# All of B's casts on GpSimd, the first group's second layer moved forward, and a fixed order for the last node blocks: a graph-network kernel on one Trainium2 core

## The chip, the cores and the metric

The kernel runs on one NeuronCore of a Trainium2 chip. A core has a matrix engine (TensorE, called PE), VectorE (DVE), ScalarE (ACT), GpSimd (POOL) and SyncE (SP, which here only starts transfers), each with its own instruction stream, which it works through in order; they meet through semaphores. Sixteen DMA engines move data between the chip's large memory (HBM) and the on-chip memory; results of PE land in PSUM[...]. The metric is the device time of a run in microseconds (us); lower is better.

## The reference

There are 6250 nodes with 128 features each (`x`) and 100000 edges from `src` to `dst`, sorted by `dst`. All arithmetic is float32.

```
h   = relu(concat(x[src], x[dst]) @ Wm1 + bm1)      # 256 wide
h   = relu(h @ Wm2 + bm2)                           # 256 wide
m   = h @ Wm3 + bm3                                 # 128 wide, a message per edge
agg = segment_sum(m, dst) / clip(count(dst), 1)     # mean of messages per node
upd = relu(concat(x, agg) @ Wn1 + bn1) @ Wn2 + bn2
out = layernorm(x + (x + upd))                      # no gain or bias, eps 1e-5
```

## The kernel before

**Tables.** `Wm1` is split in two: A = x @ Wm1[:128] and B = x @ Wm1[128:] are computed once per node rather than once per edge, and written to HBM. A row of A (`atab`) is 256 float32. A row of B (`btab`) is three bfloat16 parts whose sum is the float32 value. The nodes are 49 tiles of 128, in 13 blocks of up to four tiles. A loop (PE's order in it is written out by hand) does for each block: `turn`, which transposes x on PE (L263) into `xT`; `a_table` for pairs of tiles (product L232, copy from PSUM by ACT L241, write to HBM by SP L242); and three blocks later `b_table`. In `b_table` a pair of tiles costs: product (PE, L232), first bfloat16 part (ACT, L249), remainder `rest` (DVE, L250), second part, a cast of `rest` (L252 on POOL for the first 36 tiles, L254 on ACT for the others), third part (DVE, L255), and the write (SP, L256). The other engines are ordered by a scheduler that places instructions by its own estimate of times; where a block is marked as manually scheduled for an engine, that engine keeps the program's order.

**The node products of x.** `x @ Wn1[:128] + bn1` is also computed ahead, by `x_part`: two 128x512 products on PE per block of nodes (L316), each moved out of PSUM by ACT (L318) or DVE (L320), into the space of `xT` and `x_sb`. Four lists say where each of the 13 blocks is done: X_BESIDE between the last B products, X_BEHIND after them, X_FIRST beside the first groups of edges, X_END beside the last ones.

**Edges.** 100000 edges are 196 groups of 512. For each group `fetch` gathers 4 x 128 rows of A on POOL's queue (L412, one indirect DMA per 128 rows; they need all of `atab`) and loads the windows of B rows that the sorted destinations touch on SP's queue (L418; they need all of `btab`). There are four buffers of each. `hot` makes 0/1 matrices on DVE (L433, L436). `first_layer` adds, in PSUM, the transposed A rows (L449) and B windows times 0/1 (L455), and ACT applies the ReLU (L460). `second_layer` multiplies by Wm2 (L469) and DVE applies bias and ReLU (L471). `sums` adds the edges of a window (L478), `add_up` transposes that and DVE adds it to `acc` (L489, L494), which POOL set to zero before (L376). In PE's order a group's second layer stands after the next group's first layer.

**Nodes.** `acc` is turned into the output by 15 node blocks: the 106 odd nodes, two half blocks of 256, ten of 512, two of 256. `products` (L671, L673, L676), `hidden` (L685 to L687) two blocks ahead of `norm`. `norm` multiplies on PE (`pot`, L698, two PSUM buffers), adds 2x (`y`, DVE, L703), takes mean and variance (`bn_stats`, `bn_aggr`, L707, L708), the square root on ACT (`sd`, L710), reciprocal and shift on DVE (`rs` L712, `sh` L714), and the scaled result `o` by ACT, one instruction per 128 nodes (L718), which SP writes out (L721). `y`, `mv`, `sd` and `o` have two buffers each.

Of the kernel before, what the change touches and what calls it, by code (L numbers as in the profile page):

```python
# [27 lines left out]
def kernel(  # L28
# [122 lines left out]
    with tc.tile_pool(name="prep", bufs=1) as prep, tc.tile_pool(  # L151
# [71 lines left out]
        BLOCKS = -(-NT // 4)  # L223
        BEHIND = 3
        INDICES = 6
        LATE = BLOCKS - 4
        xu = xT, x_sb.rearrange("p t d -> p (t d)")

        def products(t0, m, k):
# [14 lines left out]
        def b_table(t0):  # L244
            m = min(2, NT - t0)
            pbt = products(t0, m, 1)
            bt = brow.tile([P, 2 * 3 * H], BF16, name="bt").rearrange("p (t c h) -> p t c h", t=2, c=3)
            rest = brow.tile([P, 2, H], F32, name="rest", bufs=2)
            nc.scalar.copy(bt[:, :m, 0], pbt[:, :m])  # L249
            nc.vector.tensor_sub(rest[:, :m], pbt[:, :m], bt[:, :m, 0])  # L250
            if t0 < 4 * LATE:
                nc.gpsimd.tensor_copy(bt[:, :m, 1], rest[:, :m])  # L252
            else:
                nc.scalar.copy(bt[:, :m, 1], rest[:, :m])  # L254
            nc.vector.tensor_sub(bt[:, :m, 2], rest[:, :m], bt[:, :m, 1])  # L255
            nc.sync.dma_start(btab[t0 * P:(t0 + m) * P].rearrange("(t p) c h -> p t c h", p=P), bt[:, :m])  # L256

        def turn(t0):
            m = min(4, NT - t0)
            pt = pp.tile([P, 4, P], F32, name="pt", tag="pp")  # L260
            for i in range(m):
                n = min(P, N - (t0 + i) * P)
                nc.tensor.transpose(pt[:, i, :n], x_sb[:n, t0 + i, :], ident[:n, :n])  # L263
            w = min(m * P, N - t0 * P)
            block = xT[:, t0 * P:t0 * P + w]
            if m == 4:
                nc.scalar.copy(block.rearrange("p (n i) -> p i n", i=4), pt)
            else:
                nc.scalar.copy(block, pt[:, 0, :w])
# [53 lines left out]
        def whole(steps):  # L323
            for _ in steps:
                pass
# [3 lines left out]

        X_BESIDE, X_BEHIND, X_FIRST, X_END = [0, 1, 2], [3, 4, 5, 6, 7, 8], [9, 12], [10, 11]
        assert sorted(X_BESIDE + X_BEHIND + X_FIRST + X_END) == list(range(BLOCKS))

        turn(0)
        for i in range(BLOCKS + BEHIND):
            if i + 1 < BLOCKS:
# [26 lines left out]
        dst_row = dst.rearrange("(o e) -> o e", o=1)  # L364
        early = [destinations(2 * k, 2, dst_row) for k in range(3)]

        turns = ExitStack()
        turns.enter_context(tc.manual_schedule(engines={ENG.DVE, ENG.Activation}))
        for b in X_BEHIND:
            whole(x_part(b, bank_pb, (nc.scalar, nc.vector)))  # L370


        PIECE = NPAD // 8
        for c in range(HC + 1):
            for k in range(8):
                nc.gpsimd.memset(acc[:, c, k * PIECE:(k + 1) * PIECE], 0.0)  # L376


        pb3 = pp.tile([P, 1], F32, name="pb3", tag="pp")
# [15 lines left out]
    with edge, tc.tile_pool(name="wk", bufs=2) as wk, tc.tile_pool(  # L395
# [136 lines left out]
        for i in range(NG + ahead + 1):  # L532
            if i == 6:
                turns.close()
            if i == 16:
                late_loads()
                none = wk.tile([16, (NG * GE - E) // 16], I32, name="none", bufs=1)
                nc.vector.memset(none, NONE)
                nc.sync.dma_start(dpad[:E].rearrange("(p e) -> p e", p=16), dst.rearrange("(p e) -> p e", p=16))
                nc.sync.dma_start(dpad[E:].rearrange("(p e) -> p e", p=16), none)  # L540
            for step, after in enumerate((20, 24, 27)):
                if i >= after and (i - after) % 8 == 0 and (i - after) // 8 < len(pieces):
                    double((i - after) // 8, step)
            if i < NG:
                nt = GT if i < NGF else LT
                firsts = load_bases(tilei[0:1, i * GT:(i + 1) * GT], nt, ENG.SP)
                if i == NGF:
                    dbs = last_destinations()
                elif i % 2 == 0:
                    dbs = early.pop(0) if early else destinations(i, min(2, NGF - i), dst_row)  # L550
                st[i] = dict(nt=nt, got=fetch(srcT[:, i, :], nt, firsts), db=dbs.pop(0))
            g = i - ahead
            if 0 <= g < NG:
                s = st[g]
                ag, bw = s.pop("got")

                def make_hot(g):
                    s = st[g]
                    hots[g], s["oh"] = hot(s.pop("db"), pbase[:, g, :], dloc[:, g, :s["nt"]], s["nt"])

                if g not in hots:
                    make_hot(g)
                oht = hots.pop(g)
            k = g - lag - 1
            if 0 <= k < NG:
                s = st.pop(k)
                if "firsts" not in s:
                    s["firsts"] = load_bases(tilei[0:1, k * GT:(k + 1) * GT], s["nt"], ENG.DVE)
                add_up(s["part"], s["firsts"], s["nt"])
            if 0 <= g < NG:  # L570
                s = st[g]
                s["h1"] = first_layer(ag, bw, oht, s["nt"])
                if first:

                    make_hot(g + 1)
                    whole(x_part(first.pop(0), bank_p2, (nc.scalar, nc.vector)))
            k = g - lag
            if 0 <= k < NG:
                s = st[k]
                s["part"] = sums(s["oh"], s["h2"], s["nt"])  # L580
            m = g - 1
            if 0 <= m < NG:
                s = st[m]
                s["h2"] = h2s[m % NH2]
                second_layer(s["h1"], s["h2"], s["nt"])
# [59 lines left out]
    with tc.tile_pool(name="nd", bufs=2) as nd, tc.tile_pool(name="nr", bufs=1) as nr, tc.tile_pool(  # L645
# [33 lines left out]
        def hidden(b, agg):  # L679
            n0, n1 = nodes_of[b]  # L680
            w = n1 - n0
            u = nd.tile([P, HC, NB], F32, name="u", bufs=4)
            for c in range(HC):
                put = pu.tile([P, NB], F32, name="put")
                nc.tensor.matmul(put[:, :w], wu1[:, 1, c * P:(c + 1) * P], agg[:, :w], start=True, stop=True)  # L685
                nc.vector.tensor_add(u[:, c, :w], put[:, :w], xu[c][:, n0:n1])  # L686
                nc.scalar.activation(u[:, c, :w], u[:, c, :w], AF.Relu)  # L687
            return u

        def norm(b, u):  # L690
# [11 lines left out]
            y = nd.tile([P, 4, D], F32, name="y")  # L702
            nc.vector.tensor_add(y[:r, :k, :], x2[:r, :k, :], pot[:r, :k, :])  # L703
            st = nd.tile([P, 4, 6], F32, name="st")
            mv = nd.tile([P, 4, 2], F32, name="mv")
# [3 lines left out]
            sd = nd.tile([P, 4], F32, name="sd")  # L709
# [4 lines left out]
            nc.vector.scalar_tensor_tensor(sh[:r, :k], mv[:r, :k, 0], -1.0, rs[:r, :k],  # L714
                                           op0=ALU.mult, op1=ALU.mult)
            o = nd.tile([P, 4, D], F32, name="o")
            for i in range(k):
                nc.scalar.activation(o[:r, i, :], y[:r, i, :], AF.Identity, bias=sh[:r, i:i + 1],  # L718
                                     scale=rs[:r, i:i + 1])
# [6 lines left out]
        FORE, BACK = 4, 2  # L726
        aggs = {b: products(b) for b in range(FORE)}
        us = {}
        for b in range(B + BACK):
            if b < B:  # L730
                us[b] = hidden(b, aggs.pop(b))
            if b >= BACK:
                norm(b - BACK, us.pop(b - BACK))
            if b + FORE < B:
                aggs[b + FORE] = products(b + FORE)


# [27 lines left out]
```

## Time and profile before

| | |
|---|---|
| time, median of 3 runs | 1451.67 us (1450.17 to 1451.95) |
| the profiled execution: its own time | 1208.8 us |
| its span, first to last instruction | 1207.0 us |
| mean granted PE clock in it | 0.996 |
| busy: PE, DVE, ACT, POOL | 1178.5, 670.4, 454.5, 804.9 us |
| loads, tables and x products (start to the first group) | 0 to 84 us |
| edge groups | 84 to about 1129 us |
| node blocks | 1129 to 1207 us |

The profile is of one execution, and that execution took 1208.8 us, not 1451.67. Durations from it can be summed against 1208.8 only. In a timeline line the first number is the start in us from the start of the span, the second the time from the first start to the last end of the merged instructions, then the engine, the line of the kernel, the operation with output and inputs, the count, and in brackets how long the engine was idle before it and what it waited for. In a table of stretches each engine has its busy time and its number of instructions, then come the granted PE clock (1.00 is full), the busy share of the DMA engines and GB/s.

### The profile page before, as it was taken

The numbers are of one execution on the slowest core, as the hardware profiler recorded it, in microseconds if no ns is written. First come the engines' busy times: TensorE is split into PE (matmuls) and PEld (weight loads), VectorE is DVE, ScalarE is ACT, GpSimd is POOL, SyncE is SP. The second block draws the span as 40 slices with busy tenths as digits, with TensorE's granted clock in tenths as the row PEclk, the third lists the DMA queues.
The fourth block names the chain that finished last, engine by engine and source line by source line (L and its number), as shares of the span: only waits on it lengthen the run. The fifth ranks groups of instructions, "written<-read, shape, count | busy, mean of one in ns | idle before, by whom it ended". The sixth has DMA issues, their size and how long they took to land. (4 is left out here: it accounts for less than half of the span.)

```text
span 1207.0 us, 32797 instructions
## 1 busy us (share of the span) xinstructions
PE 1178.5 (98%) x11196; PEld 895.0 (74%) x11197; DVE 670.4 (56%) x2080; ACT 454.5 (38%) x1163; POOL 804.9 (67%) x859
## 2 busy tenths in 40 slices
PE   7989999999999999999999999999999999999896
PEld 6747777777777777777777777777777777777565
DVE  5864555555555555555555555555555555555586
ACT  5663333333333333333333333333333333333256
POOL 8267777777777777777777777777777777673220
PEclk9999999999999999999999999999999999999999
DMA  8886666666555555555555555555555555552343
GB/s 279 293 261 174 189 180 183 189 191 177 154 151 146 152 153 153 150 152 153 149 148 152 154 154 150 149 152 146 152 153 153 152 152 150 146 148 63 97 111 105
DMA packets 173672, 193.66 MB, mean 160 GB/s; under 512 B 30844, under 2 KB 145486, under 8 KB 173488
## 3 DMA queue, kind: packets, MB, share of 16 engines
q0 software_dynamic: 37984, 103.35, 31.1%
q1 hardware_dynamic: 106956, 61.93, 17.7%
q10 hardware_dynamic: 28564, 26.27, 8.1%
q8 instruction: 90, 1.47, 0.5%
q14 instruction: 78, 0.64, 0.2%
HBM read 168.92 MB, written 22.88 MB: 159 GB/s over the span
## 5 line engine op out<-in xcount | busy, mean ns | idle before, releaser
L412 POOL DMA_INDIRECT ag<-atab,srcT x784 | 752.8, 960 | 282.4 <-issue 184.3
L469 PE MATMUL ph<-w,h 128*128 128x256 f32 x3128 | 727.5, 386 | 1.0 <-ACT x_sb L318 1.0
L469 PEld LDWEIGHTS ph<-w,h 128*128 128x128 f32 x3128 | 578.1, 190 | 152.2 <-DVE acc L494 68.2
L460 ACT ACTIVATE h<-ph,b 128x256 f32<-128x256 f32 x782 | 306.3, 474 | 675.9 <-PE ph L455 495.3
L471 DVE TENSOR_TENSOR h<-ph,nb 128x512 f32<-128x512 f32 x391 | 270.2, 692 | 413.6 <-PE ph L469 411.1
L494 DVE TENSOR_TENSOR acc<-acc,pt 128x63 f32 x782 | 171.7, 220 | 33.9 <-PE ph L455 2.6
L449 PE MATMUL ph<-ident,ag 64*128 64x64 f32 x3128 | 130.3, 223 | 0.6 <-DVE b L382 0.6
L478 PE MATMUL pg<-h,oh 128*32 128x257 f32 x1564 | 125.6, 392 | 0.0
L449 PEld LDWEIGHTS ph<-ident,ag 64*128 64x128 f32 x3128 | 113.5, 139 | 2.7 <-ACT x_sb L318 1.4
L433 DVE TENSOR_SCALAR oht<-db,pbase 128x128 bf16<-128x128 int32 x392 | 104.9, 341 | 1.3 <-PE ph L455 1.0
L489 PEld LDWEIGHTS pt<-ident,part 64*128 64x128 f32 x1173 | 50.9, 136 | 65.9 <-issue 65.2
L455 PE MATMUL ph<-oht,bw 64*128 64x128 bf16 x1564 | 76.6, 217 | 2.7 <-DMA bw<-btab 2.3
L481 ACT COPY part<-pg 128x257 f32<-128x257 f32 x196 | 76.5, 390 | 4.0 <-PE pg L478 4.0
L489 PE MATMUL pt<-ident,part 64*128 64x64 f32 x1173 | 77.8, 238 | 0.2 <-DVE acc L494 0.2
L436 DVE TENSOR_TENSOR oh<-iota_n,dloc 128x128 f32<-128x128 f32 x196 | 55.0, 280 | 20.6 <-PE pg L478 19.7
L676 POOL TENSOR_TENSOR agg<-total,rc 128x512 f32<-128x512 f32 (+2 forms) x15 | 16.0, 1070 | 69.1 <-DVE total L673 65.1
L455 PEld LDWEIGHTS <-bw 64*128 64x128 bf16 x1564 | 53.6, 96 | 3.3 <-DMA bw<-btab 2.6
L232 PE MATMUL pbt<-w,xT 128*128 128x256 f32 x196 | 48.7, 394 | 2.5 <-ACT bt L241 1.6
L478 PEld LDWEIGHTS pg<-h,oh 128*32 128x32 f32 x1564 | 30.8, 108 | 21.7 <-issue 0.8
L232 PEld LDWEIGHTS pbt<-w,xT 128*128 128x128 f32 x196 | 36.8, 197 | 10.9 <-ACT bt L241 2.8
L252 POOL CAST bt<-rest 128x512 bf16<-128x512 f32 x18 | 12.2, 686 | 27.1 <-DVE rest L250 18.0
L698 PEld LDWEIGHTS pot<-wu,u 128*128 128x128 f32 (+1 forms) x196 | 24.0, 191 | 5.5 <-issue 4.8
(109 smaller groups left out, 418.2 us busy)
## 6 DMA issues: line engine op xcount, KB each, us to landing
bw<-btab SPq DMA_DIRECT2D x782, 32.0 KB
db<-in_dst_dram ACTq DMA_DIRECT2D x194, 128.0 KB
ag<-atab,srcT POOLq DMA_INDIRECT x784
btab<-bt SPq DMA_DIRECT2D x24, 384.0 KB
atab<-bt SPq DMA_DIRECT2D x24, 256.0 KB
xd<-in_x_dram SPq DMA_DIRECT2D x12, 256.0 KB
x2tab<-xd SPq DMA_DIRECT2D x12, 256.0 KB
x_sb<-in_x_dram SPq DMA_DIRECT2D x5, 512.0 KB
```

What stands on the lines that cost most here:

```text
L232: nc.tensor.matmul(pbt[:, a, :], xT[:, (t0 + a) * P:(t0 + a + 1) * P], w1[:, k, :], start=True, stop=True)
L412: nc.gpsimd.indirect_dma_start(out=ag[:, j, :], out_offset=None, in_=atab[:, :], in_offset=bass.IndirectOffsetOnAxis(ap=idx[:, j:j + 1], a ...
L433: nc.vector.tensor_scalar(oht[:n, k, :], db[:n, k * P:(k + 1) * P], pb_cols[:n, k:k + 1], None, op0=ALU.is_equal)
L449: nc.tensor.matmul(phs[h][:, c, u * NQ:(u + 1) * NQ], ag[halves[h], u, c * P:(c + 1) * P], ident[halves[h], halves[h]], is_transpose=True, ...
L455: nc.tensor.matmul(phs[h][:, c, k * P:(k + 1) * P], bw[halves[h], k, c * P:(c + 1) * P], oht[halves[h], k, :], start=False, stop=True, ski ...
L460: nc.scalar.activation(h1[:, c, h * 2 * P:(h + 1) * 2 * P], phs[h][:, c, :], AF.Relu, bias=b1[:, c:c + 1])
L469: nc.tensor.matmul(ph2[:, a, :], h1[:, c, (j0 + a) * P:(j0 + a + 1) * P], w2[:, c, :], start=(c == 0), stop=(c == HC - 1))
L471: nc.vector.tensor_tensor(h2[:, j0:j0 + 2, :H], ph2, nb2.to_broadcast([P, 2, H]), op=ALU.max)
L478: nc.tensor.matmul(pg[j * WN:(j + 1) * WN, :], oh[:, j, :], h2[:, j, :], start=True, stop=True, skip_group_check=True)
L481: nc.scalar.copy(part[:n, :], pg[:n, :])
L489: nc.tensor.matmul(pt[:, c, :], rows, ident[halves[h], halves[h]], is_transpose=True, start=True, stop=True, skip_group_check=True)
L494: nc.vector.tensor_add(window, window, pts[j // 2][:, :, k:k + WB])
```

## The change

Four edits:

1. The second part of B is cast by POOL for all tiles (the ACT variant for the last 13 tiles goes). POOL gets the program's order from the tables on, and the zeroing of `acc` stands ahead of the loop: POOL does all 24 memsets, then all 25 casts, then the gathers. In the kernel before, 3 of the memsets stood between the first casts, and POOL had 18 casts.
2. X_BESIDE loses a block (3 to 2), X_BEHIND keeps six, X_FIRST gets the block: one block beside the first group and two (a full one and the 106 odd nodes) beside the second. There the first product is now moved by DVE and the second by ACT.
3. The second layer of group 0 comes directly after its first layer and the x block, ahead of the first layer of group 1. From group 2 on the order is as before.
4. The last node blocks: `norm` is cut into `moments` (to mean and variance), `deviation` (square root) and `scaled` (the rest). `y`, `mv`, `sd` and `o` get three buffers. For the last three blocks DVE and ACT follow the program's order, in which the moments of a block stand ahead of the scaling of the block before, and some of the `o` instructions are done by DVE.

PE, SP and the gathers execute the same instructions as before; ACT loses 7 casts of B and 3 of the last 8 `o` tiles, POOL gains the casts, DVE the tiles.

```diff
-        LATE = BLOCKS - 4
...
-            if t0 < 4 * LATE:
-                nc.gpsimd.tensor_copy(bt[:, :m, 1], rest[:, :m])
-            else:
-                nc.scalar.copy(bt[:, :m, 1], rest[:, :m])
+            nc.gpsimd.tensor_copy(bt[:, :m, 1], rest[:, :m])
...
-        X_BESIDE, X_BEHIND, X_FIRST, X_END = [0, 1, 2], [3, 4, 5, 6, 7, 8], [9, 12], [10, 11]
+        X_BESIDE, X_BEHIND, X_FIRST, X_END = [0, 1], [2, 3, 4, 5, 6, 7], [[8], [9, 12]], [10, 11]
...
+        PIECE = NPAD // 8
+        for c in range(HC + 1):
+            for k in range(8):
+                nc.gpsimd.memset(acc[:, c, k * PIECE:(k + 1) * PIECE], 0.0)
+        turns = ExitStack()
+        turns.enter_context(tc.manual_schedule(engines={ENG.Pool}))
         turn(0)
         for i in range(BLOCKS + BEHIND):
...
-        turns = ExitStack()
         turns.enter_context(tc.manual_schedule(engines={ENG.DVE, ENG.Activation}))
         for b in X_BEHIND:
             whole(x_part(b, bank_pb, (nc.scalar, nc.vector)))
-        PIECE = NPAD // 8
-        for c in range(HC + 1):
-            for k in range(8):
-                nc.gpsimd.memset(acc[:, c, k * PIECE:(k + 1) * PIECE], 0.0)
...
                 if first:
                     make_hot(g + 1)
-                    whole(x_part(first.pop(0), bank_p2, (nc.scalar, nc.vector)))
+                    for b in first.pop(0):
+                        whole(x_part(b, bank_p2, (nc.vector, nc.scalar)))
...
-            m = g - 1
-            if 0 <= m < NG:
+            m = g - 1 if g else g
+            if 0 <= m < NG and "h2" not in st[m]:
...
-            o = nd.tile([P, 4, D], F32, name="o")
-            for i in range(k):
-                nc.scalar.activation(o[:r, i, :], y[:r, i, :], AF.Identity, bias=sh[:r, i:i + 1],
-                                     scale=rs[:r, i:i + 1])
+            o = nd.tile([P, 4, D], F32, name="o", bufs=3)
+            for i, eng in zip(range(k), engines):
+                if eng is nc.scalar:
+                    eng.activation(o[:r, i, :], y[:r, i, :], AF.Identity, bias=sh[:r, i:i + 1], scale=rs[:r, i:i + 1])
+                else:
+                    eng.tensor_scalar(o[:r, i, :], y[:r, i, :], rs[:r, i:i + 1], sh[:r, i:i + 1],
+                                      op0=ALU.mult, op1=ALU.add)
...
+        with tc.manual_schedule(engines={ENG.DVE, ENG.Activation}):
+            us[B - 1] = hidden(B - 1, aggs.pop(B - 1))
+            ends = [(B - 3, [nc.scalar, nc.scalar, nc.scalar, nc.vector]), (B - 2, [nc.scalar, nc.vector]),
+                    (B - 1, [nc.vector, nc.scalar])]
+            before = None
+            for b, engines in ends:
+                y, mv = moments(b, us.pop(b))
+                sd = deviation(b, mv)
+                if before:
+                    scaled(*before)
+                before = b, y, mv, sd, engines
+            scaled(*before)
```

More of the change, by code (lines that the diff above doesn't have):

```diff
@@ L328, in bank_pb @@
             return pb.tile([P, 2, H], F32, name="pxu", tag="pbt")
-        X_BESIDE, X_BEHIND, X_FIRST, X_END = [0, 1, 2], [3, 4, 5, 6, 7, 8], [9, 12], [10, 11]
-        assert sorted(X_BESIDE + X_BEHIND + X_FIRST + X_END) == list(range(BLOCKS))
+        X_BESIDE, X_BEHIND, X_FIRST, X_END = [0, 1], [2, 3, 4, 5, 6, 7], [[8], [9, 12]], [10, 11]
+        assert sorted(X_BESIDE + X_BEHIND + sum(X_FIRST, []) + X_END) == list(range(BLOCKS))
+        PIECE = NPAD // 8
[4 more added lines that the diff above has]
+        turns.enter_context(tc.manual_schedule(engines={ENG.Pool}))
         turn(0)
@@ L688, in hidden, with moments @@
             return u
-        def norm(b, u):
+        def moments(b, u):
             n0, n1 = nodes_of[b]
@@ L701, in norm @@
             nc.sync.dma_start(x2[:r, :k], x2tab[n0:n1, :].rearrange("(t p) d -> p t d", p=r))
-            y = nd.tile([P, 4, D], F32, name="y")
+            y = nd.tile([P, 4, D], F32, name="y", bufs=3)
             nc.vector.tensor_add(y[:r, :k, :], x2[:r, :k, :], pot[:r, :k, :])
             st = nd.tile([P, 4, 6], F32, name="st")
-            mv = nd.tile([P, 4, 2], F32, name="mv")
+            mv = nd.tile([P, 4, 2], F32, name="mv", bufs=3)
             for i in range(k):
@@ L708, in norm, with deviation, scaled @@
                 nc.vector.bn_aggr(mv[:r, i, :], st[:r, i, :])
-            sd = nd.tile([P, 4], F32, name="sd")
-            nc.scalar.activation(sd[:r, :k], mv[:r, :k, 1], AF.Sqrt, bias=eps[:r])
+            return y, mv
+        def deviation(b, mv):
+            r = min(P, nodes_of[b][1] - nodes_of[b][0])
+            k = -(-(nodes_of[b][1] - nodes_of[b][0]) // P)
+            sd = nd.tile([P, 4], F32, name="sd", bufs=3)
+            nc.scalar.activation(sd[:r, :k], mv[:r, :k, 1], AF.Sqrt, bias=eps[:r])
+            return sd
+        def scaled(b, y, mv, sd, engines):
+            n0, n1 = nodes_of[b]
+            k = -(-(n1 - n0) // P)
+            r = min(P, n1 - n0)
             rs = nd.tile([P, 4], F32, name="rs")
@@ L728 @@
         us = {}
-        for b in range(B + BACK):
-            if b < B:
-                us[b] = hidden(b, aggs.pop(b))
+        for b in range(B - 1):
+            us[b] = hidden(b, aggs.pop(b))
             if b >= BACK:
-                norm(b - BACK, us.pop(b - BACK))
+                y, mv = moments(b - BACK, us.pop(b - BACK))
+                scaled(b - BACK, y, mv, deviation(b - BACK, mv), [nc.scalar] * 4)
             if b + FORE < B:
                 aggs[b + FORE] = products(b + FORE)
+        assert BACK == 2
+        with tc.manual_schedule(engines={ENG.DVE, ENG.Activation}):
[10 more added lines that the diff above has]
+            scaled(*before)
 _INS = ['x', 'src', 'dst', 'L0_gnn_Wm1', 'L0_gnn_bm1', 'L0_gnn_Wm2', 'L0_gnn_bm2', 'L0_gnn_Wm3',
```

## The prediction

> **What bounds the kernel now.** I read the engine shares first, then the table of stretches, then PE's timeline where PE is not full, then what those waits hang on.
>
> ```profile
> span 1207.0 us, 32797 instructions
> PE 1178.5 (98%) x11196; PEld 895.0 (74%) x11197; DVE 670.4 (56%) x2080; ACT 454.5 (38%) x1163; POOL 804.9 (67%) x859
> ```
>
> The table of stretches (PE, PEld, DVE, ACT, POOL busy, granted clock, DMA share, GB/s), at the change from tables to groups and at the end:
>
> ```profile
> 75.00:90.00 15.00, 12.09 (x52) 5.47 (x50) 7.44 (x23) 6.28 (x12) 11.58 (x12) 0.97 0.75 225
> 90.00:105.00 15.00, 13.62 (x121) 10.55 (x121) 6.10 (x17) 4.46 (x13) 10.94 (x13) 0.92 0.53 147
> 1190.00:1200.00 10.00, 6.84 (x54) 6.33 (x52) 7.79 (x42) 7.51 (x22) 0.00 (x0) 1.00 0.36 107
> 1200.00:1207.00 7.00, 0.00 (x0) 0.00 (x0) 1.55 (x9) 2.85 (x8) 0.00 (x0) 0.62 0.25 75
> ```
>
> PE is busy 98%: the 1045 us of edge groups are PE's, and the change leaves them alone. PE is idle 28.5 us in all; 7.2 of these wait for the first loads. What can be won lies in three places: the change from tables to groups (idle 2.9 + 1.4 us, and a clock under 1), the 2 us at 1130, and the end (3.2 us, then 7.0 us with no matmul). The change touches the first and the third.
>
> PE's timeline at the first of them, and two single microseconds of the same stretch:
>
> ```profile
> 72.61 10.55 PE L316 MATMUL pxu<-xT,wu 128*128 128x512 f32 x24
> 84.06 0.71 PE L449 MATMUL ph<-ident,ag 64*128 64x64 f32 x16 [0.57 <-DVE b L382]
> 85.91 0.23 PE L455 MATMUL ph<-oht,bw 64*128 64x128 bf16 x1 [1.13 <-DMA bw<-btab]
> 87.34 0.53 PE L455 MATMUL ph<-oht,bw 64*128 64x128 bf16 x7 [1.20 <-DMA bw<-btab]
> 87.80 2.63 PE L316 MATMUL ph<-xT,wu 128*128 128x512 f32 x4
> 93.79 3.72 PE L469 MATMUL ph<-w,h 128*128 128x256 f32 x16 [1.01 <-ACT x_sb L318]
> ```
> ```profile
> 89.00:90.00 1.00, 1.00 (x2) 0.00 (x0) 0.00 (x0) 1.00 (x3) 0.88 (x1) 0.50 0.83 207
> 91.00:92.00 1.00, 1.00 (x19) 0.80 (x16) 0.86 (x4) 0.07 (x1) 0.70 (x2) 0.50 0.49 153
> ```
>
> What stands behind that stall on SP, DVE and POOL:
>
> ```profile
> 83.05 17.13 SPq L418 DMA_DIRECT2D bw<-btab  x23
> 78.20 0.43 DVE L255 TENSOR_TENSOR bt<-rest,bt 128x256 bf16<-128x256 f32 x1 [0.64 <-ACT bt L254]
> 83.14 0.08 DVE L538 MEMSET none<- 16x22 int32 x1 [0.91 <-DMA btab<-bt]
> 66.94 1.05 POOL L412 DMA_INDIRECT ag<-atab,srcT  x1 [2.58 <-DMA atab<-bt]
> ```
>
> PE ends the x products at 83.2, and group 0's last B window lands only at 87.34. The windows are issued from 83.05, when all of `btab` is written, and the last part of `btab` left DVE at 78.63. So the stall is the chain last B product (PE, to 72.76) to `btab`, not the gathers, which run from 66.94. After the stall the granted clock is 0.50 from 89 to 92.2, so 3.2 us of matmul take twice their time. The second layer of group 0 then waits 1.01 us for a PSUM bank.
>
> DVE and ACT at the end:
>
> ```profile
> 1198.18 0.42 DVE L703 TENSOR_TENSOR y<-x,pot 128x256 f32<-128x256 f32 x1 [0.83 <-ACT o L718]
> 1200.76 0.42 DVE L703 TENSOR_TENSOR y<-x,pot 128x256 f32<-128x256 f32 x1 [1.34 <-ACT o L718]
> 1203.19 0.88 ACT L718 ACTIVATE o<-y,sh,rs 128x128 f32<-128x128 f32 x2 [0.48 <-DVE sh L714]
> ```
>
> `y` of the last two blocks waits 0.83 and 1.34 us for `o` of the block two before: with two `y` buffers the last three blocks go one after the other. The last matmul ends at 1197.2, the last `o` at 1204.07.
>
> **What the Trainium skill says.** *TensorE: Matmul & The Clock Gate*, part 1: PE falls to half its clock after an idle window of about 3.4 us, and needs one busy window to come back. The trace agrees: five thin microseconds (83 to 88, PE busy 2.1), then 0.50 for 3.2 us. The same part: ACT, DVE and GpSimd are strict FIFOs; so all gathers now stand behind the last cast. *DMA: Bandwidth & Descriptors*, the section on the anatomy of one DMA: about 2.0 us + bytes/436e3 from GpSimd's queue. No row shows a gather's landing; by this a gather of 128 KB takes an estimated 2.3 us.
>
> **The change part by part** (against the profiled 1208.8; the built order of each engine is known).
>
> *Casts, POOL, x blocks.* ACT loses 6 x 0.62 + 0.39 = 4.1 us, POOL gains 6 x 0.69 + 0.4 = 4.5 us (the half-width cast has no row; 0.4 is half plus a fixed part), DVE, PE and SP nothing. All 24 memsets first: 7.24 + 24 x 0.75 = 25.3, and the first `rest` is there at 25.7, so they cost nothing; without that cover, 0.75 us each. One x block (4 records, 10.55/24 each: 1.76 us) leaves PE ahead of the last B product, which then ends at 71.0. ACT, 13.1 of 15 us busy between 60 and 75, is lighter by more than that, so PE keeps its pace. DVE from there, in its new order: first x eviction (its product ends 72.8) to 73.5, L255 to 74.2, last L250 to 74.6, cast on POOL to 75.0, an eviction to 75.3, last L255 to 75.7: 2.9 us before 78.63. The write lands 4.4 us later as before (less, if gathers no longer share the DMA: 3.5 for the last `atab`), the last window of group 0 another 4.3: 83.5 to 84.4, take 84.0 instead of 87.34. PE, ready at 83.5 - 1.76 = 81.7, must also see DVE's last eviction and `b23` (82.4; the small memset L538, which held DVE for 0.9 us waiting for `btab`, is now behind them); group 0's first layer ends at 84.5 instead of 87.87.
>
> *Gathers.* They start at 75.3 instead of 66.94, 8.4 us late. Four take 5.06 (1.264 each), so groups 0 to 4 are there at 75.3 + 5.06 (g+1) + 2.3: 82.7, 87.7, 92.8, 97.8, 102.9. The cover is the B chain for group 0, and PE's work after it; slack 0.6 to 2.3 us, by the next part. Without it each microsecond of lateness is one on PE, once; after that the gathers draw ahead, since a group takes PE 1045 us/196 = 5.33 and POOL 5.06.
>
> *Order of the first groups.* From 84.5: x block 8 to 86.3; second layer 0 (3.7; its ReLU takes 1.6, its banks are free in time) to 90.0; first layer 1 (1.25) to 91.2; blocks 9 and 12 (1.76 + 0.45) to 93.4; first layer 2 to 94.7 (A rows 92.8); second layer 1 to 98.4, where before had 102.0. All work is then equal. That is 3.6 us; 1.6 of it is the lost half-clock window, which I take as gone: in the new order PE lacks work for some 2 us, not 4. If it stays, 2.0. First layer 3 needs rows that come at 97.8; a landing slowed by shared DMA could cost 0.5. I take 3.5.
>
> *End* (blocks counted from 0, so 12 to 14 are the last). Up to `u` of the last block nothing moves (1194.6). `y` of block 12 needs no buffer: 1194.8 to 1195.5. `sd` of 11 at 1195.5, its `o` 1196.15 to 1197.8; moments of 12 by 1197.05; `y` of 13 1197.1, moments to 1198.1; `sd` of 12 and 13 to 1198.4; `rs`, `sh` of 12 to 1198.5; ACT does three `o` to 1199.8; DVE one `o` (no row; 0.3 like the 128x128 L436) to 1198.8, `y` and moments of 14 to 1199.85, `rs`, `sh`, `o` of 13 to 1200.5, of 14 to 1201.15; ACT's last `o`, behind `sh` of 14 at 1200.85, to 1201.4. Instead of 1204.07: 2.65 us.
>
> *Sum:* 3.5 + 2.65 = 6.2; the profiled time would be 1202.6.
>
> **From there to the runs.** They are 1451.67/1208.8 = 1.20 times as long, and no row says where. If all lies in PE's time, PE runs at 0.83 of this clock. Then PE covers more of the chains: X_BEHIND and what follows to 83.5 takes 12.9 us rather than 10.7, so of the B stall (2.9 us with `b23`) about 0.7 to 1 is left to remove; the bank wait of 1.0 goes; the half-clock window (1.6) may not occur at all. Head 2.0 to 3.6. At the end, blocks 11 to 14 come about 20% further apart, `y` of 12 does not wait; the same walk from the end of its product gives 7.9 before and 6.4 after: 1.5 to 2.65. Together 3.5 to 6.2, I take 5.1: **1446.5 us**.
>
> **Rivals.** *A: the cover is already there in the runs.* With the slower PE, the stalls are mostly gone, and only the end wins: 1.5 to 2.5 us, 1449.5. For it: the factor 1.20; against: the bank wait and the `y` waits hang on ACT and DVE, not on PE's clock. *B: gathers too late.* POOL's last cast waits for DVE behind an x eviction; if that chain slips, or a gather's landing takes 5 us under the table's writes, groups 1 to 4 starve, and PE, idle in pieces, drops to half clock again. It decides from a gather start of about 81 (gain gone), and is slower than before by 0.2% from about 84: 1456. Against: DVE is 74% busy there, and PE's slower pace adds slack. *C: more,* because table writes without gathers land a microsecond sooner and no clock is lost: 9 us, 1442.5. That the change doesn't do what it says is excluded by the built order.
>
> **Chances.** A difference under 0.2% (2.9 us) is about what cannot be told from no change. Forecast 0.60 (1443.5 to 1448.7), A 0.20, B 0.10, C 0.10: faster 0.70, same 0.20, slower 0.10. The range leaves out half of C and most of B: 1441.5 to 1451.5.
>
> **What would show it.** Right: last cast at about 75, gathers from 75.3, first B window at 79 to 80, first layer 0 done before 85, clock 1.00 from 84 to 105, no PE wait for gathered rows, second layer 1 done near 98.4; at the end no wait of `y` on `o`, last `o` some 4.5 us after the last matmul. Wrong: PE waiting on rows of A in groups 1 to 4, L255 still ending past 78, a half clock after 84, or `rs` waiting on `sd` behind ACT's `o`. What would break the forecast without any of these is a run time that does not follow the profiled span.

## The result, and the profile after

The changed kernel took 1458.18 us (median of 6 runs, 1457.30 to 1459.63) against 1450.88 us of the kernel before on the same chip (1449.83 to 1451.95): a ratio of 1.0051, interval 1.0038 to 1.0064. It is 7.3 us slower. Forecast were 1446.5 us and a range that ends at 1451.5, so the sign is wrong.

The page of the changed kernel's profile; its execution took 1457.3 us:

```profile
span 1455.6 us, 32815 instructions
PE 1244.4 (85%) x11196; PEld 914.6 (63%) x11197; DVE 662.2 (45%) x2084; ACT 449.8 (31%) x1152; POOL 812.2 (56%) x866
```

Two things are to be seen. The span is now that of the runs, while the profile of the kernel before had a span of 1207.0 us at a run time of 1451. And PE, 98% busy there, is idle for 211 us here. The table of stretches, with the same columns as before, at the change from tables to groups:

```profile
75.00:90.00 15.00, 10.51 (x49) 4.98 (x47) 6.55 (x22) 2.75 (x4) 10.47 (x12) 1.00 0.58 179
90.00:105.00 15.00, 3.63 (x9) 2.95 (x10) 0.75 (x1) 2.15 (x5) 8.95 (x10) 0.50 0.36 103
```

and PE's timeline there:

```profile
82.88 0.40 PE L447 MATMUL ph<-ident,ag 64*128 64x64 f32 x6 [0.57 <-DVE xT L316]
84.05 0.40 PE L453 MATMUL ph<-oht,bw 64*128 64x128 bf16 x8
84.38 1.98 PE L312 MATMUL ph<-xT,wu 128*128 128x512 f32 x4
101.37 6.56 PE L467 MATMUL ph<-w,h 128*128 128x256 f32 x16 [15.00 <-DVE x_sb L316]
```

Group 0's first layer is over at 84.45, 3.4 us before 87.87, as the prediction had it. Then PE stops for 15.00 us, and the second layer runs at half the clock (6.56 us for what takes 3.72). PE, DVE and ACT stand still, and SP nearly so. DVE's `x_sb`, which needs only the x product that ended at 86.36, starts at 100.47, ACT's ReLU of group 0 at 100.52, and SP issues three loads of B windows between 88 and 99. The DMA engines are not full meanwhile: their busy share from 90 to 105 us is 0.36.

The line numbers are those of each kernel. In the changed kernel L447 and L453 are the first layer (gathered rows, B windows), L467 is the second layer, L410 the gathers, L416 the B windows. Without edit 1 the same lines stand four further down (L451, L457, L471). `issue` and `remote` in the brackets say that the profile names no instruction of this core that ended the wait.

So there are two questions: why an execution takes 1450 us or 1210 us, and what this stop is.

### The profile page after: what moved, and what is told of

Read it like the earlier page. It is cut to its first block, busy times and chain, and to the rows that moved or that the text cites. A ratio compares the mean times of both kernels' runs of the same rounds, so it can differ in the third digit from the quotient of the medians.

```text
span 1455.6 us, 32815 instructions
## 1 busy us (share of the span) xinstructions
PE 1244.4 (85%) x11196; PEld 914.6 (63%) x11197; DVE 662.2 (45%) x2084; ACT 449.8 (31%) x1152; POOL 812.2 (56%) x866
## 3 DMA queue, kind: packets, MB, share of 16 engines
q1 hardware_dynamic: 106956, 61.93, 14.4%
## 5 line engine op out<-in xcount | busy, mean ns | idle before, releaser
L410 POOL DMA_INDIRECT ag<-atab,srcT x784 | 755.4, 963 | 517.3 <-PE ph L453 309.4
L467 PE MATMUL ph<-w,h 128*128 128x256 f32 x3128 | 734.9, 388 | 15.9 <-DVE x_sb L316 15.0
L467 PEld LDWEIGHTS ph<-w,h 128*128 128x128 f32 x3128 | 582.5, 191 | 171.5 <-issue 74.6
L453 PE MATMUL ph<-oht,bw 64*128 64x128 bf16 x1564 | 127.4, 216 | 164.4 <-issue 147.4
L453 PEld LDWEIGHTS <-bw 64*128 64x128 bf16 x1564 | 67.3, 94 | 207.2 <-issue 171.5
L447 PE MATMUL ph<-ident,ag 64*128 64x64 f32 x3128 | 132.4, 223 | 4.8 <-issue 3.8
L447 PEld LDWEIGHTS ph<-ident,ag 64*128 64x128 f32 x3128 | 114.1, 139 | 4.2 <-issue 2.7
L250 POOL CAST bt<-rest 128x512 bf16<-128x512 f32 (+1 forms) x25 | 16.9, 683 | 34.6 <-DVE rest L249 21.7
```

The costliest lines, as they stand in the source:

```text
L410: nc.gpsimd.indirect_dma_start(out=ag[:, j, :], out_offset=None, in_=atab[:, :], in_offset=bass.IndirectOffsetOnAxis(ap=idx[:, j:j + 1], a ...
L447: nc.tensor.matmul(phs[h][:, c, u * NQ:(u + 1) * NQ], ag[halves[h], u, c * P:(c + 1) * P], ident[halves[h], halves[h]], is_transpose=True, ...
L453: nc.tensor.matmul(phs[h][:, c, k * P:(k + 1) * P], bw[halves[h], k, c * P:(c + 1) * P], oht[halves[h], k, :], start=False, stop=True, ski ...
L467: nc.tensor.matmul(ph2[:, a, :], h1[:, c, (j0 + a) * P:(j0 + a + 1) * P], w2[:, c, :], start=(c == 0), stop=(c == HC - 1))
```

## The experiments

**Two kinds of chip.** The same kernel before took 1450.9, 1431.9, 1450.7, 1431.5 and 1431.5 us in five sets of runs, each on one chip, and 1210.5 and 1209.8 us in two others. In the latter a group takes 5.27 us, in the former 6.4 to 6.5 (from the last B product of group 10 to that of group 190, over 180). I call them 5.3-us chips and 6.4-us chips. As far as the record names the chips, each set was on one of its own, so that the pace belongs to the chip, and not to the hour or to something else, is not shown; the names are labels. The profile of the kernel before that the prediction rests on has groups of 5.27 us, its 1451.67 us are those of a 6.4-us chip. The expectations name six theories. O: the new order of the first groups makes the stop. G: the late gathers do. N: it belongs to the chip, whatever the kernel. S: SyncE's own stalled instructions set the pace. B: GpSimd's unbroken run of gathers holds the others' signals back. P: the stop has a length and place of its own.

The kernel before, run as an experiment, came out at 1.0001 [0.9992, 1.0009] and 1.0002 [0.9993, 1.0011] on the two 5.3-us chips. All ratios below are against it, on the same chip. The first set of runs was expected at about 1451 us, and came out at 1210; what its expectations say of the stop was decided later, on a 6.4-us chip.

### The changed kernel on a 5.3-us chip, and its parts

Edit: none. The first repeat of it fell on a 6.4-us chip:

> The changed kernel, unchanged, beside the kernel before on one chip. The first comparison was made at 1451 against 1458 us, the last four at 1210 us for the kernel before: either this call runs at the one speed or at the other. At 1210: theory O (the stop comes with the new order): a stop of several us behind group 0, about 1215 us, ratio 1.005. Theory G (late gathers cost, the new order wins): gathers from about 77 us, PE waits 1 to 2 us in all for gathered rows of groups 1 to 3, 1207 to 1209 us, ratio 0.998, between the run without the third edit (1.0003) and the one without the first (0.9974). Theory N (the stop belongs to the slow kind of execution): no stop, ratio 0.996 to 0.999. At 1451: the stop of 15 us again under O and N, ratio 1.005.

1440.47 against 1431.86 us, 1.0054 [1.0037, 1.0071], and a stop of 14.9 us at the same place. The second fell on a 5.3-us chip:

> The changed kernel. With groups of 6.4 us: a ratio of 1.004 to 1.007 and the stop of about 15 us behind the first group's first layer, as in its two traces so far. With groups of 5.3 us: theory N expects no stop, and 1 to 3 us below the kernel before (the end's 1.8 us, and a head worth -1 to +1: ratio 0.9975 to 0.999); theory O expects the stop there too, and 6 to 9 us above (ratio 1.005 to 1.008).

It took 1204.63 against 1209.77 us: 0.9959 [0.9945, 0.9973], **5.1 us faster**. The page, the stretches and PE's timeline of this run:

```profile
span 1204.3 us, 32815 instructions
PE 1180.4 (98%) x11196; PEld 895.1 (74%) x11197; DVE 674.9 (56%) x2084; ACT 449.5 (37%) x1152; POOL 811.1 (67%) x866
```
```profile
75.00:90.00 15.00, 13.85 (x62) 7.43 (x61) 8.38 (x24) 4.90 (x9) 10.47 (x12) 1.00 0.64 189
90.00:105.00 15.00, 14.34 (x125) 10.35 (x124) 6.27 (x18) 6.01 (x15) 11.51 (x12) 1.00 0.59 155
```
```profile
84.12 0.53 PE L447 MATMUL ph<-ident,ag 64*128 64x64 f32 x10 [0.40 <-DMA ag<-atab,srcT]
84.63 0.40 PE L453 MATMUL ph<-oht,bw 64*128 64x128 bf16 x8
87.10 4.02 PE L467 MATMUL ph<-w,h 128*128 128x256 f32 x16 [0.15 <-DVE x_sb L316]
95.94 3.72 PE L467 MATMUL ph<-w,h 128*128 128x256 f32 x16
```

No stop and no half clock: PE is busy 28.2 of 30 us, where the profile of before had 25.7. That is against theory O, which had the stop here too; N had no stop, but a gain of only 1 to 3 us.

The parts were run on 5.3-us chips too. Edit 4 alone on the kernel before (the three buffers, the cut `norm`, the set order of the last blocks):

> The kernel before with the fourth edit alone (last node blocks, three buffers, set order). All theories: 1.5 to 2.7 us faster than before, ratio 0.9985, and in its trace y does not wait for o.

1208.82 us, 0.9985 [0.9977, 0.9993]: 1.8 us, and `y` of the last two blocks waits for no `o`. The changed kernel without edit 3:

```diff
-            m = g - 1 if g else g
-            if 0 <= m < NG and "h2" not in st[m]:
+            m = g - 1
+            if 0 <= m < NG:
```

> The changed kernel with the third edit undone: the second layer of group 0 again behind the first layer of group 1. Theory O: the 15 us stop is gone, 1443 to 1446 us, ratio about 0.996. Theory G: the stop stays, 1456 to 1459 us, ratio 1.005. Theory N: the stop stays.

> The changed kernel with the order of the first two groups put back (first layers of both, then their second layers). With groups of 6.4 us: theory O expects no stop and a ratio of 0.997 to 1.000; theory G (the late gathers make it) and theory N expect the stop still, and 1.004 to 1.007. With groups of 5.3 us: 1.000 to 1.001, as measured once.

1.0003 [0.9994, 1.0012] and 1.0004 [0.9994, 1.0013]: nothing is left of the gain. PE's waits from 80 to 110 us in the second of these runs (total, times, longest):

```profile
PE ph L447 <- DMA ag<-atab,srcT: 2.2, 3, 1.5
PE ph L447 <- ACT h L458: 0.9, 1, 0.9
```

In the old order PE comes to group 1's first layer before its gathered rows. Edit 3 puts 3.7 us of second layer ahead of it. Together edits 1 and 3 fit; edit 1 without edit 3 gives back what edits 2 and 4 win. In the same set of runs edit 3, with the others in place, is worth 1210.54 - 1204.63 = 5.9 us.

The changed kernel without edit 1 (so edits 2, 3 and 4):

```diff
-            nc.gpsimd.tensor_copy(bt[:, :m, 1], rest[:, :m])
+            if t0 < 4 * LATE:
+                nc.gpsimd.tensor_copy(bt[:, :m, 1], rest[:, :m])
+            else:
+                nc.scalar.copy(bt[:, :m, 1], rest[:, :m])
```

(and the 24 fills and POOL's fixed order back at their old places)

> The changed kernel with the first edit undone: ACT casts the last 13 tiles of B, gathers start near 67 us; the new order of the second layer and the x blocks stay. Theory O: the stop stays, 1456 to 1460 us. Theory G: the stop is gone, gathered rows are there 8 us earlier, 1443 to 1447 us. Theory N: the stop stays.

> The changed kernel with the casts of B shared with ScalarE as before, so that the gathers come early. With groups of 6.4 us: theory G expects no stop and a ratio of 0.997 to 0.999; theories O and N expect the stop still, 1.003 to 1.006. With groups of 5.3 us: 0.997 to 0.998, as measured once.

0.9974 on both chips ([0.9961, 0.9988] and [0.9963, 0.9985]). Edit 1, with the others in place, is worth 1206.73 - 1204.63 = 2.1 us here. So on a 5.3-us chip the edits do about what they were forecast to do.

### The same kernels on a 6.4-us chip

> The kernel before, for its trace where the groups take about 6.4 us. Ratio 1.000 by all theories. Theory O (the order of the first groups makes the stop) expects no wait of TensorE over 5 us between 80 and 120 us; theory N (the stop belongs to such executions whatever the kernel) expects one of 10 to 16 us. SyncE's register instructions between the bw loads: a mean over 100 ns as in the changed kernel's slow traces, if they belong to the chip; 29 to 37 ns if they belong to the change. If this chip gives groups of 5.3 us: no wait over 2 us, and 29 to 37 ns.

> The changed kernel with the order of the first two groups put back. With groups of 6.4 us: theory O expects no stop and a ratio of 0.997 to 1.001; theory G (late gathers make the stop) and theory N expect the stop, and 1.004 to 1.007 (N: 1.000 if the kernel before has the stop too). With groups of 5.3 us: 1.000 to 1.001, as measured twice.

> The changed kernel with the casts of B shared with ScalarE as before, so that the gathers come early. With groups of 6.4 us: theory G expects no stop and a ratio of 0.997 to 0.999; theory O expects the stop still, 1.003 to 1.006; theory N 0.997 to 0.999 with the stop in all kernels. With groups of 5.3 us: 0.997 to 0.998, as measured twice.

The ratios are 1.0003 [0.9990, 1.0016] for the kernel before, **1.0101** [1.0078, 1.0124] without edit 3, **0.9988** [0.9979, 0.9996] without edit 1. Theory O falls: without edit 3 the kernel is slower still, by more than any theory gave (1.004 to 1.007). Without edit 1 it is faster than before: edit 1, worth -2.1 us there, costs about 9 us here (1.0051 to 1.0054 less 0.9988, times 1450), though those are ratios of different chips. N is right in part: the kernel before has a stop as well, but of 7.07 us where N gave 10 to 16. G has the ratio of the kernel without edit 1 right (0.997 to 0.999), and is wrong on the stop, which it had gone. PE in the kernel before, with its own lines, and PE's longest wait without edit 1:

```profile
82.69 0.50 PE L381 MATMUL pb<-b,w 128*128 128x1 f32 x4
90.26 1.12 PE L449 MATMUL ph<-ident,ag 64*128 64x64 f32 x16 [7.07 <-DVE b L382]
```
```profile
PE ph L451 <- DVE b L384: 8.1, 1, 8.1
```

7.07 us, and 8.1 us without edit 1, against 15.0. The stop's end has a fixed relation to POOL's gathers. POOL's timeline around the end of its first unbroken run, in the kernel before on this chip:

```profile
86.22 0.95 POOL L412 DMA_INDIRECT ag<-atab,srcT  x1 [0.30 <-issue]
91.65 0.95 POOL L412 DMA_INDIRECT ag<-atab,srcT  x1 [4.48 <-PE ph L449]
```

and in the changed kernel of the first comparison:

```profile
95.97 0.96 POOL L410 DMA_INDIRECT ag<-atab,srcT  x1 [0.30 <-issue]
100.54 0.96 POOL L410 DMA_INDIRECT ag<-atab,srcT  x1 [3.62 <-remote]
```

86.22 and 95.97 are each the sixteenth gather, with which four buffers of four tiles are full; only then does POOL pause. PE goes on 4.0 and 5.4 us after the start of that sixteenth. In all six traces of 6.4-us chips with four buffers, POOL's next gather comes 4.4 to 5.4 us after the start of the sixteenth. The run of sixteen starts at 66.66 in the kernel before and at 76.89 in the changed one. Edit 1 moves it 10 us, and the end of the stop goes with it. POOL itself goes on late: PE had read the buffer that it needs next by 84.1, its sixteenth gather is over at 96.93, and the next one starts at 100.54, within 0.1 us of DVE and ACT. The kernel without edit 3 has two stops. PE's waits from 75 to 125 us:

```profile
PE ph L447 <- ACT h L458: 15.4, 1, 15.4
PE ph L312 <- DVE x_sb L316: 6.1, 1, 6.1
```

Its two first layers free two buffers in a row. So POOL makes a second unbroken run, of eight gathers, up to 109.68, and the second stop ends at 113.39.

### SyncE, or GpSimd

SP is slow in the stop. Its B-window line from 84 to 101 us, in the changed kernel on a 6.4-us chip (count: shortest/median/longest ns):

```profile
L416 SPq FUSED_REGOPS  x6: 2/690/709, 84.2 to 100.2; - x6
L416 SPq MOVE bw<-btab x6: 5/370/754, 85.7 to 100.3; - x6
```

and on a 5.3-us chip:

```profile
L416 SPq FUSED_REGOPS  x21: 37/37/42, 84.3 to 100.5; - x21
L416 SPq MOVE bw<-btab x21: 29/29/29, 84.4 to 100.6; - x21
```

Address arithmetic of 29 and 37 ns takes up to 0.75 us. To see whether that sets the pace, the windows' loads were moved to ACT's queue:

```diff
-                nc.sync.dma_start(bw[...], terms[:NQ])
+                nc.scalar.dma_start(bw[...], terms[:NQ])
...
-                firsts = load_bases(tilei[...], nt, ENG.SP)
+                firsts = load_bases(tilei[...], nt, ENG.Activation)
```

> The changed kernel with the bw loads, and the register loads of their first rows, on ScalarE's queue in place of SyncE's. With groups of 6.4 us: theory S (SyncE's own instructions stall on such a chip and set the pace of the groups) expects groups well under 6.2 us, a ratio below 0.97, and no stop; if the chip's pace has another cause (matmuls that wait for something else at the bw products), groups of 6.3 us or more and 1.000 to 1.02. With groups of 5.3 us: 0.996 to 1.01, as ScalarE has 2.4 us of work in 5.3 and gets some 2.9 us of issues, which may push h back.

1.0085 [1.0061, 1.0109], groups of 6.53 us, a stop of 12.2 us. PE stalls in the B products of 171 of 180 groups, about as many as in the changed kernel, although the register instructions, now ACT's, take 30 and 37 ns in the groups. SP's slowness is a companion of the stalls, and theory S falls.

To tell B from P, the gathers' buffers were halved:

```diff
-            ag = ld.tile([P, GT, H], F32, name="ag", bufs=4)
+            ag = ld.tile([P, GT, H], F32, name="ag", bufs=2)
```

The first unbroken run then has eight gathers. PE, ACT and POOL do the same work in the same order, DVE too but for two neighbours that change places; POOL waits for a semaphore 196 times more, once per group.

> The changed kernel with 2 buffers for gathered rows in place of 4, all else the same, so that GpSimd's first unbroken run of gathers has 8 of them in place of 16 (10.1 us in place of 20.2). With groups of 6.4 us: theory B (the burst: while GpSimd issues its first gathers back to back, the others' semaphores and SyncE crawl, and the stop ends some 4 us after the start of the last gather of the burst; so far 3.9 to 5.1 us in six traces) expects the stop's end near 77 + 8.9 + 4.5 = 90 us in place of 101, a wait of TensorE of 2 to 6 us in place of 15, and a ratio of 0.997 to 1.000 in place of 1.005. If the stop has a length or a place of its own (theory P): its end at 100 us or later, and 1.004 to 1.007. With groups of 5.3 us: 0.996 to 0.998 by both, since a gather's 5.05 us of issues and 2 to 3.6 us of landing fit in the 10.7 us between two uses of a buffer.

0.9989 [0.9978, 1.0000] on a 6.4-us chip. PE and POOL in this run:

```profile
84.52 1.98 PE L312 MATMUL ph<-xT,wu 128*128 128x512 f32 x4
90.06 3.69 PE L467 MATMUL ph<-w,h 128*128 128x256 f32 x16 [3.56 <-issue]
```
```profile
85.88 0.96 POOL L410 DMA_INDIRECT ag<-atab,srcT  x1 [0.30 <-issue]
89.24 0.96 POOL L410 DMA_INDIRECT ag<-atab,srcT  x1 [2.40 <-remote]
```

The stop ends at 90.06, where theory B had put it (90), instead of 101.4; it shrinks from 15.0 to 3.6 us. Again DVE, ACT and POOL go on within 0.1 us of each other (89.17, 89.21, 89.24). P falls. And the kernel without edit 1 with two buffers, whose run of eight is over at 77, ahead of the first group:

> The changed kernel with the casts of B shared with ScalarE as before (edits 2, 3 and 4 only), and 2 buffers for gathered rows in place of 4. Its first gathers start at 66.5 us. With groups of 6.4 us: theory B expects the first burst over at 76.6 us, ahead of the first group, so no wait of TensorE over 3 us at 81 us in place of 8.2, and a ratio of 0.992 to 0.996 (0.9988 with four buffers, less some 5 to 8 us of 1450); theory P expects the wait still, and 0.997 to 1.000. With groups of 5.3 us: 0.997 to 0.999 by both.

```profile
82.42 0.71 PE L451 MATMUL ph<-ident,ag 64*128 64x64 f32 x16 [0.57 <-DVE b L384]
88.56 3.62 PE L471 MATMUL ph<-w,h 128*128 128x256 f32 x16
```

No stop at all; but the ratio is 0.9976 [0.9964, 0.9987] and not 0.992 to 0.996. With edit 1 about 9 of the 11 us of stop come back in the run time, here hardly 2 of 8. In the traces the tables and first groups did get shorter: the last B product of group 10 ends at 151.4 us, against 158.6 without edit 1 and with four buffers, of which about 1 us is the pace of the two chips. But the ratio is to the kernel before on the same chip, and no trace of it was taken there, so where the rest went stays open. PE still waits 1.5 us for B windows in group 0, and has a clock of 0.50 from 85 to 87 us. Both were run again:

> The changed kernel with 2 buffers for gathered rows, as measured once at 0.9989 with groups of 6.4 us. With groups of 5.3 us: 0.995 to 0.998 (the changed kernel measured 0.9959 there; 5.05 us of issues and some 2 to 3.6 us of landing fit in the 10.7 us between two uses of a buffer). With groups of 6.4 us: 0.998 to 1.000.

> Edits 2, 3 and 4 with 2 buffers for gathered rows, as measured once at 0.9976 with groups of 6.4 us. With groups of 5.3 us: 0.997 to 0.999 (0.9974 with four buffers). With groups of 6.4 us: 0.996 to 0.999.

The chip was a 6.4-us one again: 0.9987 [0.9979, 0.9996] and 0.9975 [0.9967, 0.9984]. Two buffers were not measured on a 5.3-us chip.

### The 1.1 to 1.3 us in every group

On 6.4-us chips PE also stalls in nearly every group, in the middle of its B products. One group of the changed kernel, PE and POOL:

```profile
705.48 0.96 POOL L410 DMA_INDIRECT ag<-atab,srcT  x1 [0.30 <-issue]
706.34 0.22 PE L453 MATMUL ph<-oht,bw 64*128 64x128 bf16 x1
707.45 0.38 PE L453 MATMUL ph<-oht,bw 64*128 64x128 bf16 x7 [0.90 <-issue]
708.04 0.96 POOL L410 DMA_INDIRECT ag<-atab,srcT  x1 [1.60 <-PE ph L453]
```

The load of the window that the second of these products reads was issued more than two groups earlier. What is near is the last gather of a run of four, at 705.48. Over groups 20 to 184 of three traces (the changed kernel, the kernel before, and the one without edit 1 with two buffers), 464 groups have a stall over 0.4 us. In all but one of them it ends behind the fourth gather of a run, mostly 1.9 to 2.3 us after its start. This is a coincidence in time, and to test it a break was put into each run:

```diff
+                if j == 2:
+                    gap = wk.tile([P, 1024], F32, name="gap", bufs=1)
+                    nc.gpsimd.memset(gap, 0.0)
                 nc.gpsimd.indirect_dma_start(
```

(with two buffers, and POOL kept in the program's order)

> The changed kernel with 2 buffers for gathered rows and, in every group, a fill of 128x1024 by GpSimd (about 1.05 us) between its second and third gather, so that no run of gathers has more than two. With groups of 6.4 us in the kernel before: theory B (others' signals come through only when GpSimd is out of a run of gathers) expects TensorE's stalls at the bw products to become fewer and shorter, the stop at the first groups under 2 us, and groups of 6.1 to 6.4 us, which is GpSimd's own 5.05 + 1.05 and little more; if the stalls don't hang on the gathers' run, they stay at about 1.1 us a group, and groups take 7.2 to 7.6 us. With groups of 5.3 us: 6.1 to 6.2 us a group by both, a ratio near 1.13.

1.0289 [1.0270, 1.0308]; groups of 6.63 us. POOL has 0.97 us more to do in each group, and a group is only 0.22 us longer than with two buffers and no break on the same chip (6.42). The stop at the first groups is 1.7 us, under 2 as theory B had it. PE's largest waits without the break, and with it:

```profile
PE ph L453 <- issue: 135.6, 216, 1.2
```
```profile
PE pt L490 <- issue: 48.5, 24, 3.5
PE ph L456 <- issue: 25.4, 57, 1.2
PE pt L490 <- ACT part L482: 21.2, 13, 3.5
```

The stalls in the B products (L453, with the break L456) fall from 135.6 us (216 times) to 25.4 us (57 times), and new ones of up to 3.5 us come at L490. So the stalls do move with POOL's work. But 6.63 lies between what the two theories gave (6.1 to 6.4, and 7.2 to 7.6), and it is not waiting alone: the granted clock is 0.91 from 300 to 1050 us, where it was 1.00 without the break, and a second-layer matmul takes 414 ns instead of 387 on the mean, which is 0.43 us in a group's sixteen. Nor did the break do quite what it was meant to do: around 705 us POOL starts the last two gathers of one group and the first two of the next without a pause between them, so runs of four remained (48, beside 296 of two), at another place in the group. That the whole difference between the chips hangs on the gathers is therefore not shown.

## Why the prediction was wrong

**Right, and only for the profiled kind of chip.** Against the profiled 1208.8 us the sum was 6.2 us; on a chip of that kind the change brought 5.1.

- Head: 3.5 us forecast; 5.1 - 1.8 = 3.3 remain for edits 1 to 3. First layer 0 ended at 85.0 (84.5 forecast), the first B window was issued at 79.43 (79 to 80), the clock stayed at 1.00, second layer 1 ended at 99.7 (98.4).
- Gathers: forecast from 75.3, started at 77.36, since the chain of DVE and POOL ended 2 us later. PE lost 0.40 and 0.16 us to them. That edit 3 is what covers them was shown without it: 2.2 to 2.5 us of wait for rows. The landing, 2.3 us by the prediction's estimate, was not the same for all: in the kernel without edit 3 PE uses the rows 1.9 us after the end of group 0's fourth gather, and 3.4 us after that of group 1's.
- End: 2.65 us forecast, 1.8 measured with edit 4 alone. The last matmul ends at 1196.15 and the last `o` of the changed kernel at 1201.27, 5.1 us later instead of 4.5. The size that was off is DVE's: busy without a pause, it starts the last `y` at 1198.45, 2.3 us after the last matmul, where the forecast had 1.6 (1198.8 after 1197.2):

```profile
1192.19 3.96 PE L699 MATMUL pot<-wu,u 128*128 128x128 f32 x32
1200.73 0.35 DVE L734 TENSOR_SCALAR o<-y,rs,sh 128x128 f32<-128x128 f32 x1
1200.78 0.49 ACT L732 ACTIVATE o<-y,sh,rs 128x128 f32<-128x128 f32 x1 [0.20 <-ACT o L732]
```

**The step that failed** is the one from the profiled execution to the runs: "If all lies in PE's time, PE runs at 0.83 of this clock", and with it "PE's slower pace adds slack". PE does not run slower. The costliest groups of the changed kernel on a 6.4-us chip (busy, mean ns of one, idle before it):

```profile
L410 POOL DMA_INDIRECT ag<-atab,srcT x784 | 755.4, 963 | 517.3 <-PE ph L453 309.4
L467 PE MATMUL ph<-w,h 128*128 128x256 f32 x3128 | 734.9, 388 | 15.9 <-DVE x_sb L316 15.0
L453 PE MATMUL ph<-oht,bw 64*128 64x128 bf16 x1564 | 127.4, 216 | 164.4 <-issue 147.4
```

and on a 5.3-us chip:

```profile
L410 POOL DMA_INDIRECT ag<-atab,srcT x784 | 754.2, 962 | 267.1 <-issue 190.5
L467 PE MATMUL ph<-w,h 128*128 128x256 f32 x3128 | 727.8, 386 | 0.9 <-DVE h L469 0.7
L453 PE MATMUL ph<-oht,bw 64*128 64x128 bf16 x1564 | 76.0, 216 | 0.3 <-DVE oht L431 0.3
```

A second-layer matmul takes 388 and 386 ns, a gather 963 and 962, a B product 216 and 216. What differs is at the B products: 164 us more of idle time ahead of them, and 51 us more of busy time (127.4 against 76.0), since products with a stall between them overlap less (1564 of 216 ns each would be 338 us end to end). That and the stop of 15 us make up 230 of the 251 us between the two spans. Head and node blocks differ little: in the changed kernel group 0's first layer ends at 84.5 and 85.0 us, and from the last B product of group 190 to the end it is 117.8 and 116.4 us. Nor does data move slower: a DMA packet of the gathers takes 161 ns on the mean in both traces (300 to 1050 us). So the factor 1.20 was not to be spread over PE's work. It belongs to the edge groups, where PE waits.

**The gathers' price.** "Without it each microsecond of lateness is one on PE, once" took the lateness of rows for all that a late gather can cost. On a 6.4-us chip hardly a row was late: those of group 0 cost 0.29 us. What cost 8 us was *when* POOL issues, as its run of sixteen gathers came to lie over the first group instead of ahead of it. The prediction's rival B had the edit, and the wrong mechanism: its price was starved groups from a start of 81, and the loss came at a start of 76.9, while on a 5.3-us chip a start of 77.36 cost nothing to speak of. Of its signs of being wrong one appeared, the half clock after 84, as a result of the stop. Its line "what would break the forecast without any of these is a run time that does not follow the profiled span" named the weak place. The range should have been wider on the side of slower.

**The account on a 6.4-us chip:** the stop grows from 7.1 to 15.0 us, 7.9 us, and the runs are 7.3 to 8.6 us slower. The two traces are of different chips: by the last B product of group 10 the changed kernel is 7.2 us behind (166.9 against 159.7), and its node blocks are 3.1 us shorter, so that its span is only 5.1 us longer. On one and the same chip it can be seen without edit 3: its two stops add up to 21.5 us against 7.1, 14.4 more, and the runs are 15.1 us slower. What the other edits win is small beside it, and on one chip it was 0.9988 without edit 1, 1.7 us. What remains open is through what the gathers hold the others back; no experiment here looks below the instruction.

A version that beat the kernel before on both kinds of chip is the one without edit 1: 0.9974 (two 5.3-us chips) and 0.9988 (one 6.4-us chip). With two gather buffers it is 0.9975 and 0.9976 on two 6.4-us chips. On the one 5.3-us chip where it was measured, the whole change is the best, 0.9959.

## What to carry to other kernels

When the profiled span and the run times differ by a fifth, a sum against the profile says nothing on the runs until it is known which instructions or waits the difference lies in; get a profile of the kind that the runs are of, or widen the range to both signs. Where a burst of gathers on GpSimd lies can cost more than whether its rows are in time: on the 6.4-us chips it was cheapest when it was over ahead of the first group. The buffers bound its length: halving them took 11 us of a 15 us stop here, with no work added. An edit that makes work late and one that covers the lateness (edits 1 and 3) have to be judged together, on each kind of chip.

## What was not expected of the hardware

- These kernels took 1204.6 to 1210.9 us on two chips and 1427.6 to 1472.3 us on the others (medians), each with its run times within about 0.6% of one another, and the granted clock was 0.984 or more in all but one of the profiles (0.926 with the break in the gathers). The difference is mainly waits in the groups: 6.4 to 6.5 us a group instead of 5.27.
- On the 6.4-us chips, SP's register instructions between the windows' loads take about 120 ns (MOVE, 29 on the others) on the mean from 300 to 1050 us, with some near 1 us; with 117 in the kernel before, that is not of the change. The register and semaphore instructions of DVE, ACT and POOL keep their 17 to 69 ns. Moved to ACT, the same instructions took 30 ns, and PE stalled all the same.
- On a 5.3-us chip POOL issues 316 gathers from 77.36 to 480 us with no two starts more than 1.8 us apart, and PE's B products wait 0.3 us in the whole trace. In these runs a long run harms only on the other chips.
- The Trainium skill's *TensorE: Matmul & The Clock Gate*, part 1, says that the clock falls to half after an idle window of about 3.4 us. The traces agree: after the stop of 15 us the second layer of group 0 took 6.56 us for 3.72 us of work, and the granted clock was 0.50 from 90 to 105 us. After the stop of 3.56 us with two buffers the same layer took 3.69 us, at full clock.
